# Where ScalarE's side work stands in the last third of a scan round

## The chip, the core and the metric

The kernel runs on one core of one Trainium2 chip. The metric is the device time of one launch in microseconds (us). A core has TensorE (PE in the profile), VectorE (DVE), ScalarE (ACT), GpSimd (POOL) and SyncE (SP), which here only issues DMAs. Each engine works through its own instruction list in order and waits on semaphores.

## The reference, cut to what matters

The input is x of shape (8, 384, 32, 32). Layer 0 is group norm, layer norm, an input projection to two halves of 768 channels, a causal convolution of three taps, SiLU, a selective state-space scan with 16 states for each channel, a gate, an output projection and a two-layer MLP with GELU. Layer 1 is group norm and a mixture of four experts. Both add their result to x. The scan is the part around the change:

```
dt  = softplus(dt @ dt_proj_w.T + dt_proj_b)
dA  = exp(dt * A)                       # for each channel and state
dBu = dt * xc * B                       # B and C: one value for each token and state
h_t = dA_t * h_(t-1) + dBu_t            # over the 1024 tokens of an image
y_t = sum over states of h_t * C_t
```

All arithmetic is in float32.

## The kernel before

**Rounds.** The tokens are cut into 16 chunks of 512 (`NCH`), two for each image. The 768 inner channels are 6 blocks of 128 (`ND`). The 16 states are handled in 4 groups (`NG`). A round `r` is one chunk, one block and one state group, so there are 16 x 6 x 4 = 384 rounds, and a block is four rounds in a row. In a round the 128 channels x 4 states are four tiles of 128 x 512, numbered j = 0 to 3. Tiles 0 and 1 are pair A, tiles 2 and 3 pair B.

**What a round does.** ScalarE makes the four decays exp(dt * A) with `decay(r, j)` (line 734): pair A into one PSUM tile `da_A` of two banks, pair B into a PSUM tile `da_B` of one bank, which tiles 2 and 3 use in turn. GpSimd makes the driving term with `drive(r)` (line 742). VectorE runs the four recurrences with `scan(r, j)` (line 750) in the order 2, 0, 3, 1. Then `h * C` is formed by `read_out` (line 754): pair A on VectorE, which reads `da_A`, pair B on GpSimd. TensorE sums the states in `sum_states(r)` (line 776), issued one round later. When a block begins, `finish` (line 783, VectorE) multiplies the block before by its gate, and `seed` (line 769, ScalarE) starts a new PSUM sum.

Each PSUM tile exists once. So both decays of pair A of round r+1 must wait for VectorE's read-out of round r, which is the last that reads `da_A`; tile 3's decay waits for scan 2 of its own round; and tile 2's decay of the next round waits for scan 3.

**Side work.** Everything else of both layers but the last expert product runs beside the rounds: input projection, convolution, SiLU, dt, output projection, MLP, router, expert hidden layers. It is written as generators that yield before each step the engine that the step needs, its assumed cost and the number of slots to wait. A slot is one call of `side`, three in a round. `side` advances the slot counter, adds credit for TensorE and VectorE, sets ScalarE's credit, and calls `issue`, which takes ready steps in order of urgency for the engines named, until their credit is used up. Steps marked "-" (mostly DMA issues) run in every call when they are ready. So the order of all instructions on each engine is fixed when the kernel is built; nothing is reordered at run time.

Typical ScalarE side steps are the evictions of PSUM banks `h<-hid` (line 482), `r<-e_hid` (line 623, with a DMA issued behind it), `tt<-g_out` (line 459), `z<-g_in` (line 331), the convolution's first tap (lines 307 to 312), and the three activations of dt (lines 400 to 402). SiLU and GELU come in batches between two table loads, apart from `side`.

The program order on ScalarE over a round is: decay 3 of r, side work of the first and second call (or a batch), decay 2 of r+1, decays 0 and 1 of r+1, `seed` at a block's start, side work of the third call.

**The loads of dt.** A task `delta` (lines 390 to 433) makes dt of a block, writes it to DRAM and loads it back repeated over the states: `dtr_b` for pair B (two buffers), `dxr` for the drive (two buffers), `dtr_a` for pair A (one buffer). `dtr_a` of a block can be loaded only when decay 1 of the block before's last round has read the old one. The task watches for that with `while issued["A"] < last`, looks once in each slot, and after one more slot issues the two DMAs on SyncE's queue. All weight loads stand in the same queue, each waiting for TensorE to give its buffer back.

**After the rounds** the remaining projections are drained, and `experts` (from line 960) makes the last expert product with TensorE alone.

Of the kernel before, what the change touches and what calls it, by code (L numbers as in the profile page):

```python
# [34 lines left out]
ACT_FIRST, ACT_LAST, PE_SLOT, DVE_SLOT = 4.0, 1.3, 2.7, 0.6  # L35
# [17 lines left out]
def wide(ap, shape):  # L53
    return ap.to_broadcast(shape)
# [58 lines left out]
def layer0(ctx, tc, io, ident, cmean, eps, dram, x1_dram, gn1, logits, r_dram, group_norm):  # L113
# [8 lines left out]
    V, S, G, PE = nc.vector, nc.scalar, nc.gpsimd, nc.tensor  # L122
# [68 lines left out]
    def exp_ln_tables():  # L191
        S.preload_act_table_set(EXP_LN_SET)
# [38 lines left out]
    def statistics(b):  # L231
        st = p2.tile([P, NH * J, 6], F32, name="st")
        for k in range(NH):
            for j in range(J):
                if b == 0:
                    part = xt[k][:, j, :]
                else:
                    yield "-", 0, 3
                    part = pst.tile([P, T], F32, name="part")
                    nc.sync.dma_start(part, chunk_of(io["x"], b * NH + k)[:, j, :])  # L240
                    yield "-", 0, 3
                yield "DVE", 0.7, 0
                V.bn_stats(st[:, k * J + j, :], part)
        g = wp.tile([P, 2], F32, name=f"gn{b}")
        yield from group_norm(st, bank, free, p2, g)

        yield "bank", 0.2, 2
        small = bank("shift")
        PE.matmul(small[:, 0:1], lhsT=cmean, rhs=g[:, 1:2], start=True, stop=True)
        yield "ACT", 0.6, 2  # L250
        mean_w = p1.tile([P, P], F32, name="mean_w")
        S.activation(mean_w, cmean, AF.Identity, scale=g[:, 0:1])
        S.activation(g[:, 1:2], small[:, 0:1], AF.Identity, bias=g[:, 1:2], scale=-float(J))
        free()
        gn[b] = g, mean_w

    def norm(i):
        while i // NH not in gn:
            yield "-", 0, 1
        g, mean_w = gn[i // NH]  # L260
        x = xt[i]
        yield "bank", 3, 0
        mu = bank("mu")
        for j in range(J):
            PE.matmul(mu, lhsT=mean_w, rhs=x[:, j, :], start=(j == 0), stop=(j == J - 1))
        yield "DVE", 1.8, 2
        V.scalar_tensor_tensor(x, x, g[:, 0:1], wide(mu.unsqueeze(1), [P, J, T]), ALU.mult, ALU.subtract)
        free()
        sq, var = [], None
        for j in range(J + 1):  # L270
            if j < J:
                yield "ACT", 0.65, 2 * (j == 0)
                sq.append(psq.tile([P, T], F32, name="sq"))
                S.activation(sq[j], x[:, j, :], AF.Square, bias=g[:, 1:2])
            if j > 0:
                yield "PE" if var else "bank", 1, 1
                var = var or bank("var")
                PE.matmul(var, lhsT=cmean, rhs=sq[j - 1], start=(j == 1), stop=(j == J))
        yield "ACT", 1.2, 2
        S.activation(var, var, AF.Ln, bias=eps)  # L280
        S.activation(var, var, AF.Exp, scale=-0.5)
        yield "DVE", 1.8, 2
        V.scalar_tensor_tensor(x, x, g[:, 1:2], wide(var.unsqueeze(1), [P, J, T]), ALU.add, ALU.mult)
        free()
        for j in range(J):
            yield "ACT", 0.6, 2 * (j == 0)
            S.activation(x[:, j, :], x[:, j, :], AF.Identity, bias=ln_b[:, j:j + 1], scale=ln_w[:, j:j + 1])  # L287
        normal.add(i)
# [85 lines left out]
    def load_b(i, s):  # L374
        bt[i, s] = load_rows("b", i, s)

    def load_c(i, s):
        ct[i, s] = load_rows("c", i, NS + s)
# [176 lines left out]
    def in_order():  # L555
        for n in range(NCH):
            if n > 0:
                yield from (ND + d for d in range(3, 6))
            yield from range(ND)
            yield from (ND + d for d in range(3))  # L560
        yield from (ND + d for d in range(3, 6))
# [161 lines left out]
    def at(r):  # L723
        i, k = divmod(r, per)
        return i, *divmod(k, NG)
# [12 lines left out]
    def drive(r):  # L738
        i, d, s = at(r)
        issued["drive"] = r  # L740
        du[r] = pdu.tile([P, Q, T], F32, name="du")
        G.tensor_tensor(du[r], dxr[i, d], wide(bt[i, s].unsqueeze(1), [P, Q, T]), ALU.mult)  # L742
# [9 lines left out]
    def read_out(engine, r, js, h):  # L752
        i, d, s = at(r)
        engine.tensor_tensor(du[r][:, js, :], h, wide(ct[i, s].unsqueeze(1), [P, 2, T]), ALU.mult)  # L754
# [44 lines left out]
    slot, tasks, credit = [0], [], {}  # L799

    def begin(*new, rank=2):
        tasks.extend(Task(t, rank) for t in new)
# [59 lines left out]
    def drain(until=lambda: not tasks):  # L862
        while not until():
            credit.update(PE=99, ACT=99, DVE=99, batch=99)
            issue(everything)
            slot[0] += 1
        credit.update(PE=0, ACT=0, DVE=0)

    with tc.manual_schedule():
        w_in = Stream(pw_in, [("in_proj", k) for k in in_order()])  # L870
        begin(statistics(0))
        drain()
        begin(norm(0))
        drain()
        S.preload_act_table_set(SILU_SET)
        begin(*(conv(0, d, at_once=True) for d in range(ND)), x_proj(0))
        drain(lambda: len(xc) == ND)
        exp_ln_tables()
        drain()
        load_b(0, 0)  # L880
        load_c(0, 0)
        begin(delta(0, 0))
        drain()
        for s in range(1, NG):
            load_b(0, s)
            load_c(0, s)
        begin(delta(0, 1), rank=0)
        begin(*(gate(0, d) for d in range(3)))
        begin(silus(zs, gates, [(0, d) for d in range(3)]))
        begin(norm(1))  # L890
        w_out = Stream(pw_out, [("out_proj", k) for i in range(NCH) for k in range(2 * J)])
        w_1 = Stream(pw_1, [("mlp_w1", u) for i in range(NCH) for u in range(NF)])
        w_2 = Stream(pw_2, [("mlp_w2", 4 * j + 2 * half + k) for i in range(NCH) for half in range(2)
                            for j in range(J) for k in range(2)])
        seed(0, 0)
        w_e = Stream(pw_e, [("e_w1", u) for i in range(NCH) for u in range(E * J)])
        drive(0)
        for j in (2, 0, 1):
            decay(0, j)
        begin(out_lane(), rank=1.5)  # L900
        begin(hidden_lane(), rank=3)
        begin(second_lane(), rank=2.5)
        begin(expert_lane(), rank=4)

        batched = [False]

        def side(*engines, act=None):
            slot[0] += 1
            credit["PE"] = min(credit["PE"] + PE_SLOT, 4)
            credit["DVE"] = min(credit["DVE"] + DVE_SLOT, 2)  # L910
            if act is not None:
                credit["ACT"] = act + min(credit["ACT"], 0)
            issue({e: ENOUGH[e] for e in engines})

        def batch():

            ready = [t for t in tasks if t.engine == "batch" and t.ready <= slot[0]]
            batched[0] = bool(ready) and not batched[0]
            if batched[0]:
                min(ready, key=Task.urgency).resume()  # L920

        for r in range(rounds):
            i, d, s = at(r)
            k = r % per
            more = r + 1 < rounds
            plan(i, k)
            if r > 0:
                sum_states(r - 1)
            scan(r, 2)
            if more:  # L930
                drive(r + 1)
            decay(r, 3)
            batch()
            act = () if batched[0] else ("ACT",)
            side("PE", "DVE", *act, act=ACT_FIRST)
            scan(r, 0)
            scan(r, 3)
            last_token(G.tensor_copy, r, BB, du[r][:, BB, :])
            side("PE", *act)
            if more:  # L940
                decay(r + 1, 2)
            scan(r, 1)
            read_out(V, r, A, da[r, "A"])
            last_token(V.tensor_copy, r, A, da[r, "A"])
            read_out(G, r, BB, du[r][:, BB, :])
            if more:
                decay(r + 1, 0)
                decay(r + 1, 1)
            if s == 0 and r > 0:
                finish(*at(r - 1)[:2])  # L950
                seed(i, d)
            side("PE", "DVE", "ACT", act=ACT_LAST)
        sum_states(rounds - 1)
        finish(NCH - 1, ND - 1)
        begin(last_x1(), route(), rank=0)
        drain()
# [116 lines left out]
```

## Time and profile before

| | us |
|---|---|
| median of 3 runs | 4099.31 (4096.35 to 4102.39) |
| the profiled execution, its own time | 4110.87 |
| its span, first to last instruction | 4109.0 |
| rounds within the span (first to last decay, 66 to 3403) | 3337 |
| draining and the last expert product | 706 |

The profiled execution is 0.28% above the median. The time that it has outside the span is 1.9 us. The span is what the views of the profile divide up: busy time of each engine, the idle time before a group of instructions with what ended it, the waits by pair, the windows by stretch, and the timeline. A round takes 3337 / 384 = 8.7 us on average.

### The profile page before, as it was taken

How to read it: one execution, taken by the hardware profiler on the slowest of the kernel's cores; microseconds unless marked ns; L12 is line 12 of the kernel's file. 1: busy time of each engine (PE TensorE's matmuls, PEld its weight loads, DVE VectorE, ACT ScalarE, POOL GpSimd, SP SyncE). 2: the span in 40 equal slices, each digit the busy share in tenths (PEclk: the TensorE clock that was granted, in tenths of full speed). 3: DMA queues.
4: the chain of work that ended last, by engine and by line, in shares of the span. 5: the costliest groups of instructions: out<-in, count | busy, mean ns of one | idle time of the engine just before them, and what ended most of it. 6: DMA issues, size and time to landing. Idle time of an engine off the chain costs nothing. (4 is left out here: it accounts for less than half of the span.)

```text
span 4109.0 us, 35186 instructions
## 1 busy us (share of the span) xinstructions
PE 3709.2 (90%) x10294; PEld 1385.4 (34%) x10294; DVE 3032.3 (74%) x3081; ACT 2422.7 (59%) x3762; POOL 2782.5 (68%) x1070
## 2 busy tenths in 40 slices
PE   6678888999999999998999989898999899889999
PEld 2123223333333333333333333333333334334444
DVE  4888888878887878888878787878787781165552
ACT  4657676767686768676766677677767663200000
POOL 3898988788877888888878888888878881000000
PEclk8779898999999999999999999999999999899999
DMA  4444444464545454555455444555554543465552
GB/s 127 134 137 134 152 142 158 143 201 164 172 150 180 164 167 151 192 166 175 154 187 172 159 163 159 181 167 166 165 167 155 163 161 96 169 222 189 185 188 98
DMA packets 372499, 665.31 MB, mean 162 GB/s; under 512 B 40252, under 2 KB 151228, under 8 KB 370132
## 3 DMA queue, kind: packets, MB, share of 16 engines
q1 hardware_dynamic: 342352, 610.02, 45.8%
q10 hardware_dynamic: 29956, 53.05, 3.4%
q8 instruction: 83, 1.36, 0.1%
q14 instruction: 108, 0.88, 0.1%
HBM read 535.90 MB, written 127.01 MB: 161 GB/s over the span
## 5 line engine op out<-in xcount | busy, mean ns | idle before, releaser
L742 POOL TENSOR_TENSOR du<-dxr,b 128x2048 f32<-128x2048 f32 x384 | 1740.9, 4534 | 25.1 <-PE y L776 15.1
L754 POOL TENSOR_TENSOR du<-du,c 128x1024 f32<-128x1024 f32 x384 | 905.8, 2359 | 229.2 <-DVE du L750 199.7
L734 ACT ACTIVATE da_A<-dtr_a,w_a_log 128x512 f32<-128x512 f32 x768 | 527.6, 687 | 280.3 <-DVE du L754 122.1
L734 ACT ACTIVATE da_B<-dtr_b,w_a_log 128x512 f32<-128x512 f32 x768 | 527.3, 687 | 260.4 <-DVE du L750 207.2
L478 PE MATMUL hid<-tt,mlp_w 128*128 128x512 f32 x1152 | 541.5, 613 | 63.8 <-ACT h L482 46.7
L776 PE MATMUL y<-du,sel 128*32 128x512 f32 x3072 | 466.3, 642 | 134.1 <-DVE du L754 92.2
L750 DVE TENSOR_TENSOR_SCAN du<-da_B,carry,du 128x512 f32<-128x512 f32 x384 | 488.4, 1272 | 123.2 <-ACT da_B L734 114.8
L619 PE MATMUL e_hid<-xn,e_w 128*128 128x512 f32 x1080 | 519.2, 627 | 55.4 <-ACT r L623 37.9
L295 PE MATMUL g_in<-xt,in_proj 128*128 128x512 f32 x1152 | 554.7, 619 | 13.8 <-ACT xt L287 7.0
L517 PE MATMUL acc<-h,mlp_w 128*128 128x512 f32 x1152 | 543.4, 614 | 24.5 <-ACT h L493 15.9
L750 DVE TENSOR_TENSOR_SCAN du<-da_B,du 128x512 f32<-128x512 f32 x384 | 464.7, 1210 | 130.5 <-ACT da_B L734 114.0
L1026 PE MATMUL acc<-r,w_e_w 128*128 128x512 f32 x1152 | 496.6, 594 | 13.1 <-DVE r L1023 13.1
L750 DVE TENSOR_TENSOR_SCAN da_A<-da_A,carry,du 128x512 f32<-128x512 f32 x384 | 489.3, 1274 | 9.6 <-ACT da_A L734 9.0
L750 DVE TENSOR_TENSOR_SCAN da_A<-da_A,du 128x512 f32<-128x512 f32 x384 | 465.5, 1212 | 27.0 <-ACT da_A L734 25.0
L754 DVE TENSOR_TENSOR du<-da_A,c 128x1024 f32<-128x1024 f32 x384 | 470.3, 1225 | 13.2
L478 PEld LDWEIGHTS hid<-tt,mlp_w 128*128 128x128 f32 x1152 | 215.8, 193 | 366.5 <-issue 239.1
L517 PEld LDWEIGHTS acc<-h,mlp_w 128*128 128x128 f32 x1152 | 216.6, 195 | 343.9 <-issue 247.7
L295 PEld LDWEIGHTS g_in<-xt,in_proj 128*128 128x128 f32 x1152 | 210.0, 194 | 353.5 <-issue 255.1
L619 PEld LDWEIGHTS e_hid<-xn,e_w 128*128 128x128 f32 x1080 | 207.4, 199 | 356.2 <-issue 250.3
L1026 PEld LDWEIGHTS acc<-r,w_e_w 128*128 128x128 f32 x1152 | 219.6, 191 | 290.1 <-issue 287.3
L456 PE MATMUL g_out<-xc,out_proj 128*128 128x512 f32 x576 | 284.0, 641 | 32.9 <-DVE xc L783 32.9
L407 POOL TENSOR_TENSOR dtx<-dt,xc 128x512 f32<-128x512 f32 x96 | 122.1, 1272 | 217.5 <-DVE dt L404 217.5
(129 smaller groups left out, 3030.2 us busy)
## 6 DMA issues: line engine op xcount, KB each, us to landing
dxr<-dxr_dram SPq DMA_DIRECT2D x384, 256.0 KB, 4.7
mlp_w<-in_mlp_w SPq DMA_DIRECT2D x384, 192.0 KB, 2.9
dtr_b<-dtr_dram SPq DMA_DIRECT2D x192, 256.0 KB, 4.2
dtr_a<-dtr_dram SPq DMA_DIRECT2D x192, 256.0 KB, 3.2
r_dram<-r ACTq DMA_DIRECT2D x192, 256.0 KB, 3.5
r<-r_dram SPq DMA_DIRECT2D x64, 768.0 KB, 4.8
in_proj<-in_in_proj SPq DMA_DIRECT2D x192, 192.0 KB, 4.0
e_w<-in_e_w SPq DMA_DIRECT2D x192, 192.0 KB, 3.2
```

Source lines behind the costliest of these rows:

```text
L295: PE.matmul(g, lhsT=w[:, j, :], rhs=xt[i][:, j, :], start=(j == 0), stop=(j == J - 1))
L407: G.tensor_tensor(dtx, dt, xc[i, d], ALU.mult)
L456: PE.matmul(g, lhsT=w[:, d, :], rhs=xc[i, 3 * k + d], start=(k + d == 0), stop=(k == 1 and d == 2))
L478: PE.matmul(g, lhsT=w[:, j, :], rhs=tt[i][:, j, :], start=(j == 0), stop=(j == J - 1))
L517: PE.matmul(g, lhsT=w[:, n, :], rhs=hs[mine[n]], start=(k + n == 0), stop=(k == 1 and n == 2))
L619: PE.matmul(h, lhsT=w[:, j, :], rhs=xn[:, j, :], start=(j == 0), stop=(j == J - 1))
L734: S.activation(out, dtr[i, d][pair][:, j % 2, :], AF.Exp, scale=neg_a[:, d, j, s:s + 1])
L742: G.tensor_tensor(du[r], dxr[i, d], wide(bt[i, s].unsqueeze(1), [P, Q, T]), ALU.mult)
L750: V.tensor_tensor_scan(a if j < 2 else b, a, b, start, ALU.mult, ALU.add)
L754: engine.tensor_tensor(du[r][:, js, :], h, wide(ct[i, s].unsqueeze(1), [P, 2, T]), ALU.mult)
L776: PE.matmul(y[j * m:(j + 1) * m, :], lhsT=sel, rhs=h[:, j, :], start=False, stop=(s == NG - 1), tile_position=(0, j * m), skip_group_check ...
L1026: PE.matmul(acc[j], lhsT=e2[:, e, d, j, :], rhs=r[:, d, :], start=(e + d == 0), stop=(e + d == E + J - 2))
```

## The change

`side` gets a flag `tick`; with `tick=False` it neither advances the slot counter nor adds credit. The round's third call is split in two: its ScalarE part, which ticks, goes ahead of the two decays of pair A, and its TensorE and VectorE part stays where it was.

```diff
-        def side(*engines, act=None):
-            slot[0] += 1
-            credit["PE"] = min(credit["PE"] + PE_SLOT, 4)
-            credit["DVE"] = min(credit["DVE"] + DVE_SLOT, 2)
+        def side(*engines, act=None, tick=True):
+            if tick:
+                slot[0] += 1
+                credit["PE"] = min(credit["PE"] + PE_SLOT, 4)
+                credit["DVE"] = min(credit["DVE"] + DVE_SLOT, 2)
             if act is not None:
                 credit["ACT"] = act + min(credit["ACT"], 0)
             issue({e: ENOUGH[e] for e in engines})
...
             last_token(V.tensor_copy, r, A, da[r, "A"])
             read_out(G, r, BB, du[r][:, BB, :])
+            side("ACT", act=ACT_LAST)
             if more:
                 decay(r + 1, 0)
                 decay(r + 1, 1)
             if s == 0 and r > 0:
                 finish(*at(r - 1)[:2])
                 seed(i, d)
-            side("PE", "DVE", "ACT", act=ACT_LAST)
+            side("PE", "DVE", tick=False)
```

Decay 2 of the next round is issued earlier in the round than this point, so ScalarE's order becomes: decay 3 of r, side work of the first two calls, decay 2 of r+1, side work of the third call, decays 0 and 1 of r+1, `seed` at a block's start. The instructions are the same ones in the same number on every engine; their order differs on all of them, since later steps become ready in other slots.

## The prediction

> **What bounds the kernel now.** I read first how busy each engine is in the steady stretch of the rounds, by the windows view (columns: stretch, its length, then busy time of PE, PEld, DVE, ACT, POOL, then PE clock, DMA share, GB/s):
>
> ```profile
> core 0: us, PE busy (x) PEld busy (x) DVE busy (x) ACT busy (x) POOL busy (x), PEclk, DMA share, GB/s
> 800.00:3200.00 2400.00, 2218.93 (x6446) 809.58 (x6444) 1937.96 (x1933) 1704.16 (x2636) 1965.32 (x754) 0.97 0.52 168
> ```
>
> TensorE is busy 92% of the stretch, VectorE 81%, GpSimd 82%, ScalarE 71%. None is full, so the rounds are a loop of engines that wait for each other. The waits view (total us, times, longest) shows which hand-overs cost:
>
> ```profile
> DVE du L750 <- ACT da_B L734: 228.8, 235, 3.9
> ...
> ACT da_A L734 <- DVE du L754: 122.1, 80, 1.8
> ACT da_A L734 <- DVE carry L759: 110.7, 75, 1.8
> PE y L776 <- DVE du L754: 92.2, 45, 6.5
> ...
> ACT da_A L734 <- DMA dtr_a<-dtr_dram: 34.3, 10, 4.9
> DVE da_A L750 <- ACT da_A L734: 34.1, 60, 2.9
> ```
>
> VectorE waits 228.8 us for pair B's decays. Numbering the scans in their order of time, 115.6 us of it stand before scan 2 and 113.2 (100 times) before scan 3. ScalarE in its turn stands idle 232.8 us (155 times, 1.5 us each) until pair A's read-out is done. How the two hang together shows in a timeline, here round 221:
>
> ```profile
> 1968.46 0.69 ACT L734 ACTIVATE da_B<-dtr_b,w_a_log 128x512 f32<-128x512 f32 x1
> 1969.64 1.23 DVE L754 TENSOR_TENSOR du<-da_A,c 128x1024 f32<-128x1024 f32 x1
> ...
> 1970.90 1.42 ACT L734 ACTIVATE da_A<-dtr_a,w_a_log 128x512 f32<-128x512 f32 x2 [1.75 <-DVE du L754]
> ...
> 1972.26 0.67 ACT L769 ACTIVATE y<-xc,w_d_skip 128x512 f32<-128x512 f32 x1
> ...
> 1972.87 2.21 ACT L569 ACTIVATE x<-x,gn 128x512 f32<-128x512 f32 x3
> ...
> 1974.99 0.67 ACT L734 ACTIVATE da_B<-dtr_b,w_a_log 128x512 f32<-128x512 f32 x1
> ...
> 1975.69 1.28 DVE L750 TENSOR_TENSOR_SCAN du<-da_B,carry,du 128x512 f32<-128x512 f32 x1 [1.85 <-ACT da_B L734]
> ```
>
> ScalarE idles 1.75 us before pair A's decays, then does 2.21 us of side work, and so tile 3's decay is late and scan 3 waits 1.85 us. The change puts just that work into just that gap.
>
> Against it stands the load of `dtr_a`. It has one buffer, and this is SyncE's timeline at a block's end:
>
> ```profile
> 1750.61 1.17 SPq L388 DMA_DIRECT2D dtr_a<-dtr_dram  x2
> 1751.89 1.18 SPq L388 DMA_DIRECT2D dtr_b<-dtr_dram  x2
> 1753.17 0.54 SPq L217 DMA_DIRECT2D in_proj<-in_in_proj  x1
> ```
>
> Over 95 block ends the first `dtr_a` DMA is issued 0.03 us (median) after the decay that frees the buffer, both have landed after 3.9, and the next decay on pair A starts after 7.2 (lower quartile 5.6).
>
> **What the Trainium skill says.** "PSUM — Partial Sum Buffer", section "Engine vs sequencer instructions": ScalarE's, VectorE's and GpSimd's queues are strict FIFO. The timeline agrees: tile 3's decay starts 0.1 us before the side work ends, no sooner. So side work that waits for TensorE will hold pair A's decays. "DMA: Bandwidth & Descriptors", "Anatomy of one DMA": the semaphore wait of a DMA happens on the issuing sequencer before dispatch. So a load on SP stands behind the waits of those ahead. The same section's fit, 2.0 us plus bytes over 436 GB/s (made on the GpSimd path), gives an estimate of 2.6 us for 256 KB; here the trace has 2.7 to 7.2, median 3.2, for `dtr_a`, which I use. "Perfetto Trace Analysis", "Identifying the Most-Contended Engine", warns that matmul busy time is no measure of headroom; so I don't take the 92% as a full engine.
>
> **The change part by part.**
>
> *Nothing is added or removed.* The instruction lists before and after hold the same instructions. TensorE's list after the last round is the same too (758 matmuls), so the 706 us behind the rounds stay.
>
> *1. Side work into the gap: gain.* 247 of 383 rounds have side work at this place, 317 us in all or 1.3 us each. I went through them with their recorded times: side work starts when decay 2 has ended and its TensorE source is ready, pair A's decays follow, then tile 3's, each 0.7 us. Where ScalarE waits for the read-out, this takes away the wait of scan 3: 52 us in 65 rounds.
>
> *2. Side work ahead of late decays: cost.* In the other rounds decay 2 is itself late, since a batch (two table loads of 1.28 us and three activations, 4.2 us) or other side work stands before it. There pair A's decays ran at once and now wait for 0.6 to 2.2 us of work. Tile 3's decay does not move, as ScalarE's sum up to it is the same; the wait goes from scan 3 to scan 0. The loss is where the work waits for TensorE: of 213 rounds whose side work reads a matmul, in 77 that matmul ended after decay 2, 173 us in all. TensorE lags: `y` of a round starts 3.6 us (median) after the next round's first scan. Part of the 173 us is hidden by the read-out wait. Carried to scan 3, 90 us are lost in 52 rounds. Parts 1 and 2 make +38 us. Behind the waiting side work stand pair A's decays; scans 0, 3 and 1 and both read-outs wait for those.
>
> *3. `dtr_a` one slot later: cost.* `delta` tests `issued["A"]` in the ticking call. That call now runs before the decays that set it, so the test succeeds a slot later, and in SP's list `dtr_a` falls behind the two `dtr_b` DMAs at 86 of 95 block ends. At 59 another DMA stands between them too, at 40 one that waits for TensorE. The mean number of DMAs between the freeing decay and the load goes from 1.45 to 3.93. `dtr_b` waits for tile 3's decay of that round (0.7 us at best after the buffer is free), its two issues take 1.2, and being second in line costs about 0.9 (`dtr_b` takes 4.75 us from its first issue to landing in this place, `dtr_a` 3.9). Together 2.8 to 2.9. With the 87 block ends whose landing is recorded, pair A's decay would start late by the sum of max(0, shift - slack):
>
> | landing later by, us | 0 | 1 | 2 | 2.9 | 4 |
> |---|---|---|---|---|---|
> | sum of lateness, us | 9 | 27 | 68 | 120 | 194 |
>
> I take 2.9: 111 us more. Scan 2 runs in that time, which hides up to 0.55 us each, and about 70 us reach scan 0. Bounds: 20 us (shift 1.9, nothing second in line) to 150 (all behind TensorE's lag).
>
> *4. The rest.* The three activations of dt, which already wait 251.8 us in all before line 400 (on TensorE, on GpSimd, on a DMA write), stand in the moved place 21 times instead of 15. At 2.6 us each, six more are 16 us, partly in the gap; from 0 to +16. On GpSimd `dtx` (line 407) stands ahead of a drive 71 times instead of 81, of 217 us idle there, from -27 to 0, as a drive is rarely what ends a wait. PSUM banks are freed earlier: TensorE waits 46.7 us for `h` (line 482) and 37.9 for `r` (line 623), of which at most half comes back, -40 to 0. I set these against each other: 0.
>
> *Sum.* The chain of scans is held 38 + 70 = 108 us longer. Not all reaches the end: in the chain of waits from 3,076 us to the end of the rounds at 3,416, TensorE has 189 of 340 us, and where it leads, a late scan is absorbed. I pass half on: +55 us. That gives 4110.9 + 55 = 4166 for a profiled execution. The one shown lies 11.6 us above the median, so 4099.3 + 55 = **4154 us** for the median.
>
> **The rivals.**
>
> *Scan waits go, loads hold (faster).* If `dtr_a` lands less than 1 us later (18 us lost in the table) and TensorE is not behind, all 113 us before scan 3 go. Half of it is -57 or so: 4043; with part of the losses, 4060 to 4085. For it: the 232.8 us of idle time are real and in the right place. Against: SP's list, and TensorE's lag. It decides at a shift of about 1.5 us together with under 50 us of waits for matmuls.
>
> *TensorE absorbs everything (no change).* If TensorE leads nearly always, scans that are later by 0.3 us a round cost nothing: 4095 to 4107. Against it: TensorE waits 92.2 us for pair A's read-out and others like it.
>
> *Loads and side work add up (much slower).* If all loads land 4 us later (+185) and side work's 173 us of waits come through, the sum is some 300 to 350, and passed on by half or more: 4250 to 4350. For it: a late chain delays evictions too, and TensorE then waits for banks.
>
> That the change does nothing can be excluded: in the built order nothing but `seed` is left between pair A's decays and tile 3's.
>
> **How the numbers follow.** About 0.2% (8 us) can be told from no change. Forecast 0.58, much slower 0.11, absorbed 0.09, faster 0.22. The likeliest case alone, with the bounds of part 3 and a pass-on of a third to all, is 4110 to 4240. The range reaches into the faster case to 4070; left out are its lower half and most of the much slower case.
>
> **What would show it.** Right: ScalarE's wait for the read-out (232.8 us) falls below 160; scan 3's wait (113.2) falls below 60, while VectorE's wait for `da_A` (34.1) grows past 150; ScalarE's wait for the DMA `dtr_a` (34.3) grows past 100; the first `dtr_a` issue comes 2 to 3 us after the freeing decay. Wrong: `dtr_a` waits stay under 50 us, or TensorE's busy share of the stretch rises over 93%; then the faster rival holds. If the waits move as said and the time stays, the pass-on was wrong.

## The result and the profile after

The changed kernel takes **4136.24 us** (median of 5 runs, 4129.40 to 4140.09) against 4099.31 us (5 runs, 4095.64 to 4102.65): ratio 1.0089, 95% interval 1.0075 to 1.0103, or 37 us more. The profiled execution has a span of 4138.3 us, 29.3 more than before (it lies 3.9 us above its median, the one before 11.6). The rounds, from the first to the last decay (66.2 to 3435.0), take 3369 us, 32 more. Behind the last decay lie 703 us, 2 fewer than before, with 1551 matmuls recorded and 1553 before. So all of the loss is in the rounds.

The steady stretch again, by the windows view (length, busy time of PE, PEld, DVE, ACT, POOL, PE clock, DMA share, GB/s):

```profile
core 0: us, PE busy (x) PEld busy (x) DVE busy (x) ACT busy (x) POOL busy (x), PEclk, DMA share, GB/s
800.00:3200.00 2400.00, 2215.58 (x6454) 819.73 (x6453) 1927.27 (x1924) 1700.89 (x2635) 1962.33 (x748) 0.96 0.50 167
```

No engine has become the bound. PE, DVE, ACT and POOL all do a little less in the same 2400 us, VectorE 0.6% less.

TensorE's mean granted clock is lower in this profile (0.939, before 0.948), so slower matmuls could be a cause by themselves. They aren't: between the first and the last decay TensorE is busy 2985.6 us, 13 fewer than before, and idle 383 us, 45 more. What has changed is who waits for whom (waits view: total us, times, longest):

```profile
DVE da_A L750 <- ACT da_A L734: 357.9, 214, 5.7
...
ACT da_A L734 <- DMA dtr_a<-dtr_dram: 155.6, 88, 5.8
PE y L776 <- ACT y L769: 132.3, 36, 10.1
...
ACT tt L459 <- PE g_out L456: 109.7, 37, 5.7
DVE du L750 <- ACT da_B L734: 108.9, 146, 3.3
...
DVE dt L404 <- ACT dt L402: 78.7, 56, 6.0
...
ACT da_A L734 <- DVE carry L759: 38.4, 31, 1.8
...
ACT da_A L734 <- DVE du L754: 27.8, 25, 1.8
```

Four waits of the kernel before, for comparison:

```profile
DVE dt L404 <- ACT dt L402: 159.3, 81, 6.0
...
DVE xc L314 <- ACT edge L312: 71.3, 35, 7.8
...
PE y L776 <- ACT y L769: 24.2, 16, 4.4
...
ACT tt L459 <- PE g_out L456: 21.1, 10, 5.7
```

ScalarE's idle time before pair A's decays that waits for the read-out falls from 232.8 to 66.2 us (the last two lines of the view after). VectorE's wait for pair B's decays halves; the part before scan 3 is gone (113.2 to 0) and the part before scan 2 stays (115.6 to 108.9). In exchange VectorE waits 357.9 us for pair A's decays, 34.1 before. The decays themselves wait 155.6 us for `dtr_a`, 34.3 before. Two lines come from waits that the prediction did not name: TensorE waits 132.3 us for `seed`, which was 24.2, and ScalarE 109.7 us for the output projection's matmul, which was 21.1.

Both kinds of wait in one place, the end of round 195. First ScalarE's timeline (start, us, engine, line, operation, idle time before it with its releaser):

```profile
1783.94 1.42 ACT L734 ACTIVATE da_A<-dtr_a,w_a_log 128x512 f32<-128x512 f32 x2 [1.03 <-DVE carry L759]
1785.29 0.67 ACT L734 ACTIVATE da_B<-dtr_b,w_a_log 128x512 f32<-128x512 f32 x1
1785.90 0.57 ACT L459 COPY tt<-g_out 128x512 f32<-128x512 f32 x1
1787.76 0.69 ACT L734 ACTIVATE da_B<-dtr_b,w_a_log 128x512 f32<-128x512 f32 x1 [1.28 <-DVE du L750]
1789.80 0.58 ACT L459 COPY tt<-g_out 128x512 f32<-128x512 f32 x1 [1.35 <-PE g_out L456]
1791.76 0.69 ACT L734 ACTIVATE da_A<-dtr_a,w_a_log 128x512 f32<-128x512 f32 x1 [1.37 <-DMA dtr_a<-dtr_dram]
1793.46 0.69 ACT L734 ACTIVATE da_A<-dtr_a,w_a_log 128x512 f32<-128x512 f32 x1 [1.01 <-DMA dtr_a<-dtr_dram]
```

Then SyncE's, over the same time:

```profile
1785.99 1.17 SPq L388 DMA_DIRECT2D dtr_b<-dtr_dram  x2
1787.25 0.54 SPq L217 DMA_DIRECT2D out_proj<-in_out_proj  x1
1787.84 1.16 SPq L388 DMA_DIRECT2D dtr_a<-dtr_dram  x2
```

The decays at 1783.94 free `dtr_a` at 1785.36. SyncE's next entry is `dtr_b`, which waits for the decay of tile 3 that ends at 1785.96; a weight load follows, and `dtr_a` is issued 2.5 us after its buffer is free. Meanwhile ScalarE has an eviction in front of pair A's decays and stands 1.35 us for its matmul. Then the two decays wait for their two loads, 1.37 and 1.01 us. In this round the load comes last, so the eviction's wait is hidden behind it.

Over the 95 block ends the first `dtr_a` issue comes 2.5 us (median) after the freeing decay, where it came after 0.03 us in the kernel before. The last landing that is recorded comes after 7.65 us instead of 3.9.

### The profile page after: what moved, and what is told of

Read it like the earlier page. It is cut to its first block, busy times and chain, and to the rows that moved or that the text cites. A ratio compares the mean times of both kernels' runs of the same rounds, so it can differ in the third digit from the quotient of the medians.

```text
span 4138.3 us, 35154 instructions
## 1 busy us (share of the span) xinstructions
PE 3693.4 (89%) x10294; PEld 1394.5 (34%) x10294; DVE 3025.6 (73%) x3081; ACT 2419.1 (58%) x3762; POOL 2783.9 (67%) x1070
## 4 chain that ended last, share of the span: by engine, by line
PE 56%; ACT 22%; DVE 7%; DMA 7%; issue 4%; SPq 2%; POOL 1%; ACTq 0%; DVEq 0%; POOLq 0%
PE acc L1028 12%; PE acc L517 8%; PE hid L478 7%; PE e_hid L619 7%; PE g_in L295 6%; PE y L776 5%; PE g_out L456 5%; ACT da_A L734 4%; DMA dtr_a<-dtr_dram 4%; ACT da_B L734 3%; DVE da_A L750 3%; DVE du L750 2%; PE g_dt L396 2%; SPq L388 2%; ACT L192 2%
## 5 line engine op out<-in xcount | busy, mean ns | idle before, releaser
L734 ACT ACTIVATE da_A<-dtr_a,w_a_log 128x512 f32<-128x512 f32 x768 | 529.4, 689 | 264.6 <-DMA dtr_a<-dtr_dram 155.6
L776 PE MATMUL y<-du,sel 128*32 128x512 f32 x3072 | 458.9, 642 | 224.6 <-ACT y L769 132.3
L619 PE MATMUL e_hid<-xn,e_w 128*128 128x512 f32 x1080 | 504.9, 612 | 45.7 <-ACT r L623 22.0
L1025 DVE TENSOR_TENSOR r<-r,spread 128x1536 f32<-128x1536 f32 x64 | 112.4, 1757 | 193.7 <-DMA r<-r_dram 185.0
```

The lines of the kernel that those rows point to most:

```text
L619: PE.matmul(h, lhsT=w[:, j, :], rhs=xn[:, j, :], start=(j == 0), stop=(j == J - 1))
L734: S.activation(out, dtr[i, d][pair][:, j % 2, :], AF.Exp, scale=neg_a[:, d, j, s:s + 1])
L776: PE.matmul(y[j * m:(j + 1) * m, :], lhsT=sel, rhs=h[:, j, :], start=False, stop=(s == NG - 1), tile_position=(0, j * m), skip_group_check ...
L1025: V.tensor_tensor(r4, r4, wide(spread[i][:, :, e, :].unsqueeze(1), [P, J, TT, P]), ALU.mult)
```

## The experiments

All times stand against the kernel before, run on the same chip (its medians there: 4097.5 for the first four, 4098.6 for the next four, 4099.5 for the last two). Two candidates stood at the start: the late load of `dtr_a`, and the place of the side work itself. A third came out of the runs: the output projection.

**The load back in its old slot.** The changed kernel, without the waiting slot ahead of the load. Against the changed kernel only SyncE's list differs.

```diff
         while issued["A"] < last:
             yield "-", 0, 1
-        yield "-", 0, 1
         pair = dtr[i, d]["A"] = p1.tile([P, 2, T], F32, name="dtr_a")
```

> The changed kernel with one waiting slot taken out ahead of the dtr_a load, so that the load stands ahead of dtr_b again, as in the kernel before; the order of ScalarE, VectorE, GpSimd and TensorE stays that of the changed kernel. Theory (the late load is most of the cost): 4085 to 4110 us, ScalarE's wait for the DMA dtr_a back under 60 us (from 156), TensorE's wait for the seed (132 us) down with it to under 60. Rival (side work that waits for TensorE ahead of pair A's decays is the cost): 4125 to 4140 us, scan 0 still waits 300 us or more for da_A.

Measured: 4085.65 us, ratio 0.9967 (0.9955 to 0.9979), 50 us under the changed kernel. Its waits (line numbers behind the load are one lower here):

```profile
DVE da_A L749 <- ACT da_A L733: 291.2, 194, 5.7
...
ACT tt L458 <- PE g_out L455: 115.4, 38, 5.7
PE y L775 <- ACT y L768: 109.1, 31, 8.8
...
ACT da_A L733 <- DMA dtr_a<-dtr_dram: 36.1, 20, 4.7
```

The late load is a real cost. But the wait for `seed`, expected to fall under 60, is still 109.1, and scan 0 still waits 291.2 us. Something else holds ScalarE there, and the second line says what it waits for.

**Only the load late.** The kernel before, with one slot more ahead of the load.

```diff
         while issued["A"] < last:
             yield "-", 0, 1
-        yield "-", 0, 1
+        yield "-", 0, 2
         pair = dtr[i, d]["A"] = p1.tile([P, 2, T], F32, name="dtr_a")
```

> The kernel before with one more waiting slot ahead of the dtr_a load and nothing else: ScalarE's, VectorE's and GpSimd's orders are those of the kernel before, and dtr_a stands behind dtr_b at 91 of 95 block ends. Theory (late load): 4130 to 4150 us, ScalarE waits 120 us or more for the DMA dtr_a. Rival (side work ahead of the decays is the cost): 4099 to 4110 us, as the lateness is absorbed.

Measured: 4200.99 us, 1.0254 (1.0234 to 1.0273), 103 us more, twice the upper end of what was expected. The wait for the load:

```profile
ACT da_A L734 <- DMA dtr_a<-dtr_dram: 292.4, 124, 6.7
```

Here the first issue comes 3.8 us (median) after the freeing decay and the last recorded landing after 9.35, so a slot is worth more in this order than in the changed one.

**Only the split.** The third call is split, but both parts stay behind the decays.

```diff
-            side("ACT", act=ACT_LAST)
             if more:
                 decay(r + 1, 0)
                 decay(r + 1, 1)
             if s == 0 and r > 0:
                 finish(*at(r - 1)[:2])
                 seed(i, d)
+            side("ACT", act=ACT_LAST)
             side("PE", "DVE", tick=False)
```

> The third call split in two as in the change, but both parts behind pair A's decays and the seed, where the one call stood. Theory (place and late load matter, the split doesn't): 4095 to 4105 us, scan 3 still waits about 110 us for da_B. Rival (the split's other choice of steps for each slot is the cost): 4120 to 4140 us.

Measured: 4055.34 us, 0.9895 (0.9877 to 0.9913): 42 us faster, which no theory had expected. No call has moved across the decays (though the order of steps differs on all engines), and the waits of before are still there:

```profile
DVE du L750 <- ACT da_B L734: 228.5, 231, 4.0
...
DVE dt L404 <- ACT dt L402: 154.0, 73, 6.0
...
DVE xc L314 <- ACT edge L312: 65.5, 31, 7.8
```

**Early, except beside a batch.** The load early (the edit of the first experiment, not repeated here), and side work ahead of pair A's decays only in rounds without a batch; otherwise behind `seed`.

```diff
+            if not batched[0]:
+                side("ACT", act=ACT_LAST)
-            side("ACT", act=ACT_LAST)
             if more:
                 decay(r + 1, 0)
                 decay(r + 1, 1)
             if s == 0 and r > 0:
                 finish(*at(r - 1)[:2])
                 seed(i, d)
+            if batched[0]:
+                side("ACT", act=ACT_LAST)
```

> The changed kernel with the early load, and with the side work moved ahead of pair A's decays only in rounds without a batch; in rounds with one it stays behind the seed. Theory (late load most of the cost; in batch rounds the decays are late already and the move only shifts a wait): within 10 us of the kernel with the early load alone, 4080 to 4110 us. Rival (side work ahead of late decays is the cost): 15 us or more below the kernel with the early load alone.

Measured: 4147.33 us, 1.0108 (1.0088 to 1.0127), 62 us over the early load alone. Both expectations missed: taking the move out of the rounds with a batch, which the prediction counted among those that lose, makes the kernel slower. TensorE's, VectorE's and GpSimd's lists are the same as with the early load alone; in SyncE's the load stands elsewhere at 36 block ends. The time is no better than with no move at all and the same three lists (4138.77 us, the experiment on the output projection below; the intervals overlap). So in that order the move in rounds without a batch gains nothing that can be measured, and the gain comes with the batch rounds.

**The move alone.** The split kernel, with the ScalarE call moved ahead of the decays, but with both flags that the call polls set before it: `finish` ahead of it, and `issued["A"]` already counted. The lists of TensorE, VectorE, GpSimd and SyncE are those of the split kernel; only ScalarE's differs.

```diff
+            if s == 0 and r > 0:
+                finish(*at(r - 1)[:2])
+            if more:
+                issued["A"] = r + 1
+            side("ACT", act=ACT_LAST)
             if more:
                 decay(r + 1, 0)
                 decay(r + 1, 1)
             if s == 0 and r > 0:
-                finish(*at(r - 1)[:2])
                 seed(i, d)
-            side("ACT", act=ACT_LAST)
             side("PE", "DVE", tick=False)
```

> The split kernel with the ScalarE part ahead of pair A's decays, where nothing else moves: finish is issued and the flag for dtr_a is set ahead of that call, so that every waiting step sees in this slot what it sees in the split kernel. TensorE's, VectorE's and GpSimd's orders are those of the split kernel. Theory (the place itself is worth next to nothing; what the change costs beside the late load is that the output projection sees finish a slot later): 4045 to 4070 us, against 4055 for the split kernel. Rival (side work ahead of pair A's decays is what costs): 4075 to 4095 us, with 250 us or more of waits of scan 0 for da_A.

Measured: **4012.82 us**, 0.9791 (0.9778 to 0.9805). The move as such is worth 42.5 us, and more than its own theory had. Its waits:

```profile
DVE da_A L750 <- ACT da_A L734: 248.4, 182, 6.3
...
DVE dt L404 <- ACT dt L402: 112.0, 63, 6.0
...
DVE du L750 <- ACT da_B L734: 84.5, 117, 2.5
...
PE y L776 <- ACT y L769: 61.2, 38, 5.5
```

Scan 0 waits 248.4 us for its decay instead of 32.8 in the split kernel, and the kernel is still faster. What it gets in return is more than the scans: scans 2 and 3 wait 144 us less. VectorE's step of dt waits 42 us less for ScalarE. The convolution's second step at line 314 waits 34 us for ScalarE where it waited 98. TensorE stands idle 279 us in the rounds instead of 317, and its busy time there is the same (2967 and 2965 us).

**Only the output projection late.** The split kernel, side work behind the decays and load early, with one slot more ahead of the output projection. The lists of TensorE, VectorE and GpSimd are those of the changed kernel.

```diff
         while (i, ND - 1) not in finished or i - 1 in tt:
             yield "-", 0, 1
+        yield "-", 0, 1
         t = p1.tile([P, J, T], F32, name="tt")
```

> The split kernel with one more waiting slot ahead of the output projection and nothing else: the side work stays behind pair A's decays, the load of dtr_a stays early. Theory: 4075 to 4095 us. Rival (the place costs): 4050 to 4062 us.

Measured: 4138.77 us, 1.0097 (1.0081 to 1.0112), 83 us over the split kernel, which waits 21.8 us at this eviction and 32.7 us for `seed`. Both expectations missed; the late output projection costs at least twice what was expected. Lines are one higher here:

```profile
ACT tt L460 <- PE g_out L457: 91.8, 31, 5.7
...
PE y L777 <- ACT y L770: 89.3, 17, 8.5
```

Here no side work stands in front of pair A's decays, and yet both new waits of the changed kernel are there. So the late output projection brings both without help from the place. (The place adds something to the wait for `seed`: 61.2 us in the move alone, 32.7 in the split kernel.) The early-load kernel has the same lists on all engines but ScalarE and differs by the place: it is 53 us faster. That is a second measure of what the place is worth. In this pair slower matmuls have a part: TensorE's busy time in the rounds is 3003 us here and 2967 there, at mean granted clocks of 0.936 and 0.946.

**The split, with ScalarE in its second part too.**

```diff
             side("ACT", act=ACT_LAST)
-            side("PE", "DVE", tick=False)
+            side("PE", "DVE", "ACT", tick=False)
```

> The split kernel, whose second part may also issue ScalarE steps with the credit left. Theory (the split gains because ScalarE steps that become ready through a TensorE or VectorE step of the same call wait for the next slot): 4085 to 4105 us, the gain is gone. Rival (it gains because ScalarE's steps are taken ahead of the others, whatever comes later): 4045 to 4065 us.

Measured: 4096.05 us, 0.9998 (0.9989 to 1.0007). The gain of the split is gone. So it came, as far as this one kernel tells, from this: a ScalarE step that becomes ready through a TensorE or VectorE step of the same call has to wait for the next slot once the call is split. Which of those steps carries the 42 us was not found.

**The move in eight of 24 rounds.** The move alone, but only in those rounds of a chunk that were picked for the waits before scan 3.

```diff
-            side("ACT", act=ACT_LAST)
+            early = k in (0, 1, 3, 12, 18, 19, 20, 23)
+            if early:
+                side("ACT", act=ACT_LAST)
...
                 seed(i, d)
+            if not early:
+                side("ACT", act=ACT_LAST)
```

> As the kernel in which the place alone moves, but ahead of the decays only in 8 of the 24 rounds of a chunk, those where the trace of the split kernel shows scan 3 waiting for tile 3's decay while the matmul that the side work reads is done (30 us of such waits in all). Theory: 10 to 20 us below the split kernel, 4035 to 4048. Rival (these waits are absorbed elsewhere): 4050 to 4062 us.

Measured: 4064.98 us, 0.9921 (0.9904 to 0.9938). It is 52 us slower than the move in all rounds, and no faster than the move in none (4055.34 us; the intervals overlap). The rival's range is missed too, by 3 us. The theory behind the choice falls: what the move is worth can't be read off the waits of the scans, round by round. Why the move in a part of the rounds gains nothing is open, here and in the kernel with batches left out.

**The changed kernel with `finish` ahead of the call.** The output projection then starts as before; the load is still late.

```diff
+            if s == 0 and r > 0:
+                finish(*at(r - 1)[:2])
             side("ACT", act=ACT_LAST)
             if more:
                 decay(r + 1, 0)
                 decay(r + 1, 1)
             if s == 0 and r > 0:
-                finish(*at(r - 1)[:2])
                 seed(i, d)
```

> The changed kernel with finish ahead of the ScalarE part, so that the output projection starts in the slot of the kernel before; the load of dtr_a stays a slot late. TensorE's, VectorE's, GpSimd's and ScalarE's orders are those of the kernel in which the place alone moves (4013 us); only SyncE's list differs. Theory (the costs add): 4013 + 50 = 4063 us, 4050 to 4085, and ScalarE waits some 150 us for the DMA dtr_a. Rival (a late load costs what it did in the kernel before, 103): 4105 to 4125 us.

Measured: 4076.41 us, 0.9952 (0.9935 to 0.9970), 60 us under the changed kernel and 64 over the move alone, from which only SyncE's list differs.

```profile
ACT da_A L734 <- DMA dtr_a<-dtr_dram: 159.8, 93, 5.3
...
PE y L776 <- ACT y L769: 65.7, 43, 5.9
...
ACT tt L459 <- PE g_out L456: 27.4, 17, 5.7
```

The waits for the output projection (109.7) and for `seed` (132.3) are down, and the wait for the load is what it was. The two costs can be taken apart.

**`seed` between pair A's decays.** The move alone, with `seed` one decay earlier.

```diff
             if more:
                 decay(r + 1, 0)
-                decay(r + 1, 1)
             if s == 0 and r > 0:
                 seed(i, d)
+            if more:
+                decay(r + 1, 1)
```

> The kernel in which the place alone moves, with the seed between pair A's two decays, so that it is 0.7 us sooner and decay 1 as much later at a block's start. Theory (TensorE's 61 us of waits for the seed are on the path): 4000 to 4010 us. Rival (scan 1 is the next wait, or the wait is absorbed): 4010 to 4020 us.

Measured: **4003.62 us**, 0.9776 (0.9762 to 0.9790), the lowest of all, 2.2% under the kernel before. From the move alone it differs by 9 us, which is small: the two intervals overlap. TensorE's wait for `seed` is halved, from 61.2:

```profile
PE y L776 <- ACT y L769: 30.7, 19, 4.5
```

## Why the prediction came out right, and which of its parts did not

The direction and the size were right: +55 us was forecast, +37 came. But the runs give another sum, and that the total fits is in part luck:

| what the change does | from | us |
|---|---|---|
| splits the call: chains within a call are cut | split − before | −42 |
| ScalarE's side work ahead of pair A's decays | move alone − split | −42.5 |
| output projection sees `finish` one slot later | early load − move alone | +73 |
| `dtr_a` loaded one slot later | changed − early load | +50.5 |
| sum | | +39 |

Other pairs of kernels give −53 for the place, +60 and +83 for the output projection, and +64 and +103 for the load. So the prices depend on the order around them (for the place, −42.5 and −53 are hardly apart, given that the runs of one kernel spread by some 10 us), and the table is one path through them, which closes by its making (but for 2 us by which the kernel before differs between chips). Against it the forecast had, after its half, +19 for the place, +35 for the load and 0 for the rest. The place was 61 us too high, the rest 31 too low and the load 15 too low. Two errors of one sign and a large one of the other leave 15 us in sum.

*Parts 1 and 2, the place: the sign was wrong.* The mechanism is there as told: the wait of scan 3 is gone, ScalarE's wait for the read-out is down by 72%, scan 0 has the new wait. The failed step is the sum of −52 and +90. It counted two scans of a chain and priced side work there only as an obstacle to decays. What other engines gain when side work comes sooner was taken up in part 4, for `dtx` and the PSUM banks, and was set against costs to make 0. VectorE also runs steps that wait for that side work, and these were not priced. In the changed kernel line 404 waits 78.7 us for ScalarE, 159.3 before, and line 314 waits 27.7, 121.2 before. With VectorE's list unchanged, from the split kernel to the move alone, they fall from 154 to 112 and from 98 to 34. Those waits stood in the waits view of the kernel before. That rounds with a late decay 2 lose 90 us is not borne out for those with a batch: leaving them out cost 62 us. That these other steps make the whole gain is argued; that the place as such gains 42 to 53 us is shown.

*Part 3, the load: right in kind, too small.* The list order, the wait for tile 3's decay and the wait for `dtr_a` came as described. The issue came 2.5 us later, within the 2 to 3 of its check, where the sum had 0.7 + 1.2 = 1.9. The landing came 3.7 us later instead of 2.9: being further back in the queue cost 1.2 instead of 0.9. The forecast passes half of 70, or 35 us, on to the end; 50 were measured. The prediction's own table has about 174 us of lateness at 3.7; less the 9 that were there and the 41 that it let scan 2 hide, 124 reach scan 0, and half of that is 62, against 50 measured in this order and 64 and 103 in two others. So the under-sized term is the shift. "DMA: Bandwidth & Descriptors" of the Trainium skill, section "Anatomy of one DMA", has the wait on the issuing sequencer before dispatch; SyncE's timeline above agrees: `dtr_b` is issued at 1785.99, 0.03 us after tile 3's decay has ended, and the weight load and `dtr_a` stand behind it.

*Part 4, "the rest" at 0: the step that left out two terms.* They are +73 and −42. The prediction noticed that `delta` polls a flag in the ticking call which is set behind it, and did not ask who else polls. The output projection polls `finished`, which `finish` sets behind the moved call. Its matmuls start a slot later. Of the 576 that are recorded over the 16 chunks, 146 started in round 0 of a chunk (counted from 0) and 35 in round 3; now none start in round 0 and 232 in round 3. TensorE has nothing of them in round 0, where its idle time over the chunks goes from 38 to 87 us (68 with the load early). In round 3, where it is idle for only 2 us, the evictions on ScalarE wait 77 of their 109.7 us for it and stand before pair A's decays. Of the 132.3 us of waits for `seed`, 87 stand in round 1. The time shows it in its place. Counted from one start of scan 2 to the next, a chunk's round 3 takes 9.6 us on average, 6.6 before; it takes 9.6 in the kernel with only the output projection late, and 6.5 in the split kernel and the move alone. Over sixteen chunks that is 48 us. Round 0, where 9.5 stand against 7.9, belongs to the load: 7.8 with the load early, 9.7 with `finish` first and the load late. A reading in this part was off too: of the 251.8 us before line 400 the waits view gives no cause for 86.7, and the one DMA that it names is a weight load (5.3 us), not a write.

*The pass-on and the rivals.* The half was never tested by itself, as the terms that it multiplied were wrong. Of the rivals, "scan waits go, loads hold" was nearer to the truth of the place than the forecast. With the load early it gives 4085.65, just over the upper end of its 4060 to 4085; with the flags mended it gives 4012.82, below what it allowed. "TensorE absorbs everything" is refuted: with ScalarE's list alone changed by the whole move the time moved by 42 and 53 us, with SyncE's alone by 50, 64 and 103.

*The checks named.* Read-out wait 66.2 (under 160), scan 3's wait 0 (under 60), wait for `da_A` 357.9 (over 150), wait for `dtr_a` 155.6 (over 100), issue after 2.5 us (2 to 3), TensorE's share 92% (not over 93). All came as said, and still did not tell whether the place costs or gains. They show that waits moved, not what each is worth.

**Open:** which steps carry the split's gain; why the move in a part of the rounds gains nothing; how much of the place's gain runs through the evictions that give TensorE its banks.

## What to carry to other kernels

When a call that polls is moved ahead of what sets its flags, list every flag it polls: each one behind it is now seen a slot late, and here two of them cost 60 and 50 us or more while the move itself was a gain of 42. Price a moved step by everything that waits for it on other engines, not only by what it stands in front of. Where an order is fixed by a build-time planner, separate the parts by making the other engines' lists identical; the same slot of one load was worth 50, 64 and 103 us in three orders.

## What was not expected of the hardware

A DMA issued later by 2.5 us landed later by 3.7: 256 KB of `dtr_a` took 4.4 us (median) from issue to landing where they took 3.2 before, with two `dtr_b` loads and often a weight load just ahead of them in the queue. The early-load kernel, with the same lists but for the place of this load, has 3.4. So in these runs the load's own duration depends on its place in the list, and not only its start.
